# Two-layer graph network on one core: the first dense product and ten chunks of x placed inside the stage that reads R, R in another chunk order, part of the dense R gathered in hop 1

## Chip, cores and metric

The kernel runs on one core of a Trainium2 chip. The metric is the device time of one execution in microseconds (us); lower is better. All data is fp32. The engines are named as in the profile: PE (TensorE, matmul; PEld is its weight load), DVE (VectorE), ACT (ScalarE), POOL (GpSimd), SP (SyncE, which only issues DMAs here).

## The reference

x is 8 x 2048 x 128 (batch, node, feature). adj, called R below, is 2048 x 2048, symmetric in its pattern, with the diagonal full and otherwise about 0.4% of entries set at random, so a 128 x 32 tile of it has few rows that are not zero.

```
# layer 0
sj = x @ w_j;  si = x @ w_i
res = si[:, :, None] + sj[:, None, :] + adj[None] * w_r + g_b
x = layernorm(x + einsum('bij,bjd->bid', res, x) @ weight + bias)
# layer 1: two hops over adj, used as A1 and as A2
x1 = einsum('bnf,nw->bwf', x, adj)
x2 = 2 * einsum('bnf,nw->bwf', x1, adj) - x
out = layernorm(x + relu(concat[x, x1, x2, x1, x2] @ Theta1 + bias))
```

Three products with R are needed: one with R transposed (layer 0), two with R (the hops of layer 1). The outer sum si + sj + b has low rank and is added as a product with nine rows.

## The kernel before

**Blocks.** The 2048 nodes are 16 chunks of 128. A chunk of x or of a result is 128 partitions x 1024 numbers (8 batches x 128 features, 0.5 MiB); a row chunk of R is 128 x 2048 (1 MiB). ND = 4: chunks 0 to 3 are called dense. In layer 0 they are multiplied with the full transposed R, kept on chip in `at4`. For chunks 4 to 15 (and for all 16 in both hops) only the rows that matter are fetched: an index list per 32-column tile ("T", four lists for a chunk) and for the rest ("H", three lists for a chunk). A list is one gather of up to 128 rows of 4 KiB by POOL (`gather`, line 475), so a chunk takes seven gathers. The matching pieces of R have to be gathered too.

**Stage R (lines 294 to 314).** Row chunks arrive in a ring of three buffers `am` (parts of `rc`). For a chunk, PE transposes it in 16 blocks (`row_groups`, 221), ACT writes the result times w_r to `at_of(n)`: `at4` for dense chunks, else one of six buffers in `Y` and `rct`. DVE reduces both forms to masks (`mask_rows`, `mask_columns`). Transposed chunks 4 to 15 are stored to `rr_d` (`store_rt`, 241), 512-byte pieces; chunks 4 to 10 inside the stage, 11 to 15 after it (632). In every second row chunk one chunk of x is transposed (`x_t`) and multiplied with the weights (`y_of`): eight of the 16, the result in `Y`. SP issues from one queue in order: `pump` (199) takes loads from the list `todo`, rows at most three ahead and x at most six ahead.

**After stage R (630 to 661).** For x chunks 8 to 15 PE does `x_t`, `y_of` and two of the 16 steps of the first dense product (`full_rows(0, ...)`, 285; a step is two 128x512 matmuls). In between DVE turns the masks into lists: `ranked(0)` in step n = 9, `candidates` and eight rounds of maxima in step 10, `lists_end(0)` in step 13. `lists_end(0)` gives the T lists, and POOL's first gathers follow it: `get_job` (495) issues one job (R for one chunk and one kind, T four gathers, H three), `keep_job` (510) masks what arrived into `rct` and `rc` on DVE. Jobs run in the order of line 490: T of chunks 6 to 15, 4, 5; H of 4 to 15; then T and H of chunks 0, 1, 2, 3 straight from adj. They pass through a ring of four slots in `st`. The copies of adj's columns to `rr_d` and the 16 stores of `Y` to `y0_d` go through SP's queue after the last chunk of x.

**Dense products 1 to 3 (740 to 809).** PE runs `full_rows(1..3)`. DVE runs the second list extraction, whose rounds (`end_round`, 624) hold one keep and one get each; `lists_end(1)` after the second step of dense product 2 gives the H lists. 22 jobs (all 12 T, ten H: 78 gathers) are issued before the first gather of rows of `y0_d` (`get_rows(0, ND, "T", y0_d)`, 791).

**Sparse loop of layer 0 (812 to 833).** For each chunk c of 4 to 15: seven gathers of `y0_d` into a ring of twelve buffers in `Y`, one keep and one get (here R of the dense chunks, eight jobs of 28 gathers, in c = 4 to 11), own block, rank-9 product, `listed`, then DVE's `z_add` and `layernorm`, and `make_u` of the chunk before, which stores to `u_d`.

**Hops (836 to 903).** Two loops over 16 chunks, with seven gathers each from `u_d` (hop 1) or `y_d` (hop 2); `end` (847) closes a chunk. Every engine keeps its own program order.

Of the kernel before, what the change touches and what calls it, by code (L numbers as in the profile page):

```python
# [11 lines left out]
ALU = mybir.AluOpType  # L12
# [6 lines left out]
def kernel(  # L19
# [22 lines left out]
    P = 128  # L42
# [7 lines left out]
    ND = 4  # L50
# [7 lines left out]
    T_ORDER = list(range(6, NC)) + [4, 5]  # L58
    assert D == P and B == 8 and NC == 16
# [115 lines left out]
    ats = [Y[:, n:n + 2].rearrange("p c b f -> p (c b f)") for n in range(8, NC, 2)]  # L175
    ats += [rct[:, n * N:(n + 1) * N] for n in range(2)]

    def at_of(c):
        t = at4[:, c] if c < ND else ats[(c - ND) % 6]
        return t.rearrange("p (j i) -> p j i", i=P)  # L180

    xin = {}
    todo = []
    for m in range(8):
        todo += [("a", 2 * m), ("x", m)] if m else [("a", 0), ("a", 1), ("x", 0)]
        if m:
            todo.append(("a", 2 * m + 1))
    todo += [("x", n) for n in range(8, NC)] + [("c", c) for c in T_ORDER]
    done = {"a": 0, "x": 0}

    def load_x(c, t):
        sp.dma_start(out=t, in_=x[:, c * P:(c + 1) * P, :].rearrange("b p f -> p b f"))
        return t
# [4 lines left out]

    def pump():
        while todo and (  # L200
            todo[0][0] == "c" or todo[0][1] < done[todo[0][0]] + {"a": 3, "x": 6}[todo[0][0]]
        ):
            what, n = todo.pop(0)
            if what == "c":
                copies([n])
            elif what == "a":
                sp.dma_start(out=am[n % 3], in_=adj[n * P:(n + 1) * P, :])
            else:
                xin[n] = load_x(n, ring[:, n % 6])

    turn = [0]
    turns = [6, 7, 0, 1]
# [8 lines left out]
    def row_groups(n, gs):  # L221
        a, at = am[n % 3], at_of(n)
        for g in gs:
            b = transposes([a[:, (4 * g + i) * P:(4 * g + i + 1) * P] for i in range(4)])
            act.activation(at[:, 4 * g:4 * g + 4, :], b, AF.Copy, scale=wr)
        if gs[-1] == 3:
            done["a"] = n + 1

    def mask_rows(n):
        dve.tensor_reduce(  # L230
            mk[:, n, :], am[n % 3].rearrange("p (t f) -> p t f", f=TW), AX.X, ALU.max,
            apply_absolute_value=True,
        )

    def mask_columns(c):
        dve.tensor_reduce(
            mkt[:, :, QT * c:QT * c + QT], at_of(c).rearrange("p j (t f) -> p j t f", f=TW), AX.X,
            ALU.max, apply_absolute_value=True,
        )
# [4 lines left out]
    def x_t(n):  # L244
        t = []
        for h in range(2):
            b = transposes([xin[n][:, h * HB + i, :] for i in range(4)])
            d = trp[:, (2 * n + h) % 3]
            act.copy(d, b)
            t.append(d)  # L250
        done["x"] = n + 1
        return t
# [40 lines left out]

    pump()
    for m in range(8):
        n = 2 * m
        mask_rows(n)
        row_groups(n, [0, 1, 2, 3])
        pump()
        if ND <= n < NC - 5:  # L300
            store_rt(n)
        if n - 1 >= ND:
            mask_columns(n - 1)
        mask_rows(n + 1)
        row_groups(n + 1, [0, 1])
        xt = x_t(m)
        row_groups(n + 1, [2, 3])
        pump()
        if ND <= n + 1 < NC - 5:
            store_rt(n + 1)  # L310
        y_of(m, xt)
        if n >= ND:
            mask_columns(n)
# [179 lines left out]
    got, kept = [0], [0]  # L493

    def get_job():
        if got[0] == len(jobs):
            return
        what, c = jobs[got[0]]
        s = st[:, got[0] % 4 * BD:]
        got[0] += 1  # L500
        for n, i in enumerate(columns(c, what)):
            if c >= ND:
                gather(
                    s[:, n * 2 * P:(n + 1) * 2 * P], rr_d[c - ND].rearrange("n m f -> n (m f)"), idx,
                    i, N,
                )
            else:
                gather(s[:, n * P:(n + 1) * P], adj128, idr, i, N * NC)

    def keep_job():  # L510
        if kept[0] == got[0]:
            return
        what, c = jobs[kept[0]]
        s = st[:, kept[0] % 4 * BD:]
        kept[0] += 1
        m = 2 if c >= ND else 1
        hc = has[:, columns(c, what)[0]:columns(c, what)[0] + QT]
        for k in range(m):
            if m == 1 or k == 1:
                to = rc[:, c * W:(c + 1) * W]  # L520
            else:
                to = rct[:, (c - ND) * W:(c - ND + 1) * W]
            of = s[:, k * P:]
            if what == "T":
                step = m * P + TW
                dve.tensor_mul(
                    to[:, 0:P].rearrange("p (t f) -> p t f", t=QT),
                    strided(of, QT, step, TW),
                    hc[:, :, None].to_broadcast([P, QT, TW]),
                )  # L530
            else:
                step = m * P + 64
                dve.tensor_mul(
                    to[:, P:2 * P].rearrange("p (t f) -> p t f", t=2), strided(of, 2, step, 64),
                    hc[:, 0:2, None].to_broadcast([P, 2, 64]),
                )
                i = NT + 2 * NC + c
                dve.tensor_scalar(
                    to[:, 2 * P:3 * P], of[:, 2 * m * P:2 * m * P + P], has[:, i:i + 1], None,
                    op0=ALU.mult,  # L540
                )
# [31 lines left out]

    par = [1]

    def acc_pair():
        par[0] ^= 1
        return bank[2 * par[0]:2 * par[0] + 2]
# [52 lines left out]
    acc0 = acc_pair()  # L631
    for c in range(NC - 5, NC):
        store_rt(c)
    for n in range(8, NC):
        xt = x_t(n)
        pump()
        y_of(n, xt)
        if n == 9:
            ranked(0)
        if n in (8, 10, 12):  # L640
            s_rows(2 * (n - 8))
        if n == 10:
            candidates()
            for r in range(8):
                round_of(lists, cand, r)
        if n == 13:
            lists_end(0)
            get_job()
            get_job()
            encode2()  # L650
            get_job()
            get_job()
        if n == 14:
            split2()
        if n == 15:
            candidates2()
            end_round(0)
        full_rows(0, acc0, range(2 * (n - 8), min(2 * (n - 7), 15)))
    assert not todo
    s_rows(12)  # L660
    full_rows(0, acc0, [15])

    zs = {}

    def load_z(c):
        zs[c] = load_x(c, ring[:, 3 + c % 3])

    load_z(0)
    load_z(1)
# [46 lines left out]
    homes = [ring[:, 0], ring[:, 1], ring[:, 2], spare, ring[:, 4], ring[:, 5], ring[:, 3]]  # L716
    homes = [homes[c % 7] for c in range(12)] + [slab(k) for k in range(4)]
# [24 lines left out]
    for r in range(1, 4):  # L742
        end_round(r)
    for c0 in range(0, NC, 4):
        column_sums(c0)
    full_rows(1, acc1, range(4, 6))
    make_ub()
    full_rows(1, acc1, range(6, 12))
    for r in range(4, 8):
        end_round(r)  # L750
    si_t(0)
    rank9(0, acc0)
    z_add(acc0, zs[0])
    full_rows(1, acc1, range(12, NC))
    si_t(1)
    rank9(1, acc1)

    acc2 = acc_pair()
    full_rows(2, acc2, range(0, 2))
# [4 lines left out]
    z_add(acc1, zs[1])  # L764
    layernorm(zs[0], "0_0")
    full_rows(2, acc2, range(2, 8))
# [4 lines left out]
    full_rows(2, acc2, range(8, 12))  # L771
    make_u(0, zs[0], x1t[0], u_of[0])
    load_z(3)
    for _ in range(3):
        keep_job()
        get_job()
    full_rows(2, acc2, range(12, NC))
    si_t(2)
    rank9(2, acc2)
    z_add(acc2, zs[2])  # L780

    acc3 = acc_pair()
    full_rows(3, acc3, range(0, 4))
    make_u(1, zs[1], x1t[1], u_of[1])
    load_z(4)
    for _ in range(3):
        keep_job()
        get_job()
    layernorm(zs[2], "0_2")
    full_rows(3, acc3, range(4, 8))  # L790
# [3 lines left out]
    for _ in range(2):  # L794
        keep_job()
        get_job()
    full_rows(3, acc3, range(8, 12))
    get_rows(0, ND, "H", y0_d)
    keep_job()
    keep_job()  # L800
    get_rows(0, ND + 1, "T", y0_d)
    full_rows(3, acc3, range(12, NC))
# [30 lines left out]
    assert kept[0] == len(jobs)  # L833


    def hop(i, src, order, there, between):
# [51 lines left out]
        for k, c in enumerate(order):  # L888
            rows(k, "H")
            if k > 1:  # L890
                begin(k)
            fetch(k + 2)
            if k > 0:
                rows(k + 1, "T")
            listed(i, c, accs[k], "H")
            end(c, accs[k])

    hop(
        1, u_d, list(range(NC)), range(12, NC),
        lambda: make_u(NC - 1, zs[NC - 1], x1t[NC - 1], u_of[NC - 1]),  # L900
    )
    homes[0:5] = homes[5:10]
    hop(2, y_d, list(range(5, NC)) + list(range(5)), range(5, NC), lambda: None)
# [94 lines left out]
```

## Time and profile before

| | us |
|---|---|
| median of 3 runs | 811.46 (810.09 to 814.63) |
| profiled execution, its own time | 812.94 |
| its span in the profile | 811.0 |
| stage R, last row chunk's mask starts | 94.95 |
| first gather by POOL | 143.19 |
| first gather of rows of y0_d | 254.20 |
| first chunk of the sparse loop added up (z_add, c = 4) | 283.80 |
| last chunk of the sparse loop added up (c = 15) | 432.91 |
| first H gather of hop 1 | 453.94 |
| hop 2, about | 640 to 798 |

Over the span PE is busy 722.5 us (89%), POOL 442.2 (55%), DVE 411.2 (51%), ACT 191.4 (24%); 258.10 MB are moved. POOL's busy time leaves out a gap of about 0.30 us after each gather in which it issues; one gather of about 1.0 us holds POOL for 1.30 us. "DMA" is the mean busy share of the core's 16 DMA engines; by the way it is measured it can pass 1.

### The profile page before, as it was taken

The page shows a single profiled execution, that of the slowest core. Times are in us where ns is not written, and L with a number is a line of the kernel's source. Part 1 is how long each engine was busy: PE and PEld are TensorE (multiplying, and loading weights), DVE is VectorE, ACT ScalarE, POOL GpSimd, SP SyncE. Part 2 cuts the span into 40 slices and gives each one's busy share as a digit, 9 for nine tenths or more (in the row PEclk, how much of TensorE's full clock was granted, in tenths as well). Part 3 has the DMA queues.
Part 4 walks back from the last instruction along what each step waited for, and adds up shares of the span by engine and source line. Part 5 has one row for each costly group of instructions (what it writes and reads, how often), then busy time and mean ns, then how long its engine had stood idle before and what let it go on. Part 6 is the DMA issues. An engine that isn't in the chain of part 4 may idle for free. (4 is left out here: it accounts for less than half of the span.)

```text
span 811.0 us, 10100 instructions
## 1 busy us (share of the span) xinstructions
PE 722.5 (89%) x3566; PEld 373.6 (46%) x3566; DVE 411.2 (51%) x589; ACT 191.4 (24%) x440; POOL 442.2 (55%) x432
## 2 busy tenths in 40 slices
PE   4965699999999998987998799999999899999992
PEld 4865666634345443433444344434444445553441
DVE  4766778698644354543654000000000377777775
ACT  3965644400121232321332100000000011111111
POOL 1000000777577777777644566566663777777640
PEclk9988899999999999999999999999999999999997
DMA  7999999999237799999999899999998799999982
GB/s 251 337 329 316 313 301 316 329 377 399 68 113 257 239 327 351 323 364 328 367 366 323 294 388 382 359 377 344 356 358 344 266 361 351 349 383 379 372 303 71
DMA packets 170036, 258.10 MB, mean 318 GB/s; under 512 B 17409, under 2 KB 122266, under 8 KB 167928
## 3 DMA queue, kind: packets, MB, share of 16 engines
q0 software_dynamic: 49280, 146.52, 49.2%
q1 hardware_dynamic: 97936, 85.21, 32.7%
q10 hardware_dynamic: 22760, 25.63, 9.0%
q8 instruction: 30, 0.49, 0.2%
q14 instruction: 30, 0.25, 0.1%
HBM read 239.01 MB, written 58.72 MB: 367 GB/s over the span
## 5 line engine op out<-in xcount | busy, mean ns | idle before, releaser
L67 POOL DMA_INDIRECT Y<-y_d,idx x196 | 212.0, 1082 | 81.8 <-issue 29.9
L67 PE MATMUL bank<-Y,rc 128*32 128x512 f32 (+2 forms) x896 | 215.7, 607 | 16.1 <-DMA Y<-u_d,idx 12.9
L67 POOL DMA_INDIRECT st<-rr_d,idx x84 | 85.7, 1020 | 172.6 <-DVE rown L67 139.7
L67 POOL DMA_INDIRECT Y<-u_d,idx x112 | 111.7, 998 | 76.7 <-issue 29.1
L67 PEld LDWEIGHTS bank<-Y,rc 128*32 128x32 f32 (+2 forms) x896 | 60.2, 128 | 168.5 <-issue 87.2
L67 PE MATMUL bank<-Y,at 128*128 128x512 f32 x256 | 115.1, 603 | 0.0
L67 PE MATMUL bank<-Y,rct 128*32 128x512 f32 (+2 forms) x336 | 74.8, 604 | 12.9 <-DMA Y<-y_d,idx 12.9
L67 PEld LDWEIGHTS bank<-Y,at 128*128 128x128 f32 x256 | 48.0, 192 | 58.2 <-issue 58.1
L67 DVE TENSOR_REDUCE s<-sq 128x4 f32<-128x512 f32 x64 | 43.9, 686 | 59.4 <-ACT sq L67 59.4
L67 PE MATMUL bank<-ident,rc 128*128 128x128 f32 (+2 forms) x316 | 45.1, 307 | 27.3 <-DMA rc<-in_adj_dram 27.3
L67 ACT ACTIVATE sq<-ring 128x512 f32<-128x512 f32 x54 | 34.0, 630 | 141.2 <-DVE ring L67 94.0
L67 DVE COPY ring<-bank 128x512 f32<-128x512 f32 x10 | 6.9, 692 | 109.0 <-PE bank L67 109.0
L67 PE MATMUL bank<-ring,rd 128*128 128x512 f32 x132 | 62.2, 594 | 0.0
L67 DVE TENSOR_TENSOR ring<-bank,ring 128x512 f32<-128x512 f32 x32 | 21.7, 689 | 67.0 <-PE bank L67 67.0
L67 PEld LDWEIGHTS bank<-ident,rc 128*128 128x128 f32 (+2 forms) x316 | 39.8, 162 | 29.8 <-issue 26.2
L67 DVE TENSOR_REDUCE st<-rc 128x64 f32<-128x2048 f32 x16 | 36.5, 2284 | 31.9 <-DMA rc<-in_adj_dram 31.9
L67 PE MATMUL bank<-th,at 128*128 128x128 f32 x384 | 47.7, 277 | 1.8 <-ACT at L67 1.7
L67 PEld LDWEIGHTS bank<-th,at 128*128 128x128 f32 x384 | 45.3, 192 | 7.9 <-issue 4.2
L67 PEld LDWEIGHTS bank<-Y,rct 128*32 128x32 f32 (+2 forms) x336 | 20.3, 128 | 59.5 <-issue 30.8
L67 ACT COPY ring<-bank 128x512 f32<-128x512 f32 x34 | 19.9, 585 | 114.6 <-PE bank L67 114.6
L67 PE MATMUL bank<-wx,trp 128*128 128x130 f32 x256 | 37.9, 293 | 6.9 <-ACT sraw L67 4.0
L67 PEld LDWEIGHTS bank<-ident,ring 128*128 128x128 f32 x256 | 32.6, 152 | 15.8 <-issue 14.8
(133 smaller groups left out, 788.2 us busy)
## 6 DMA issues: line engine op xcount, KB each, us to landing
rc<-in_adj_dram SPq DMA_DIRECT2D x16, 1024.0 KB, 11.8
ring<-in_x_dram SPq DMA_DIRECT2D x32, 512.0 KB, 9.1
rr_d<-in_adj_dram SPq DMA_DIRECT2D x12, 1024.0 KB, 10.1
ring<-y_d SPq DMA_DIRECT2D x17, 512.0 KB, 8.1
rr_d<-Y SPq DMA_DIRECT2D x8, 1024.0 KB, 9.9
y_d<-Y SPq DMA_DIRECT2D x16, 512.0 KB, 11.5
u_d<-ring ACTq DMA_DIRECT2D x12, 512.0 KB, 7.4
out_dram<-ring ACTq DMA_DIRECT2D x11, 512.0 KB, 8.9
```

The lines of the kernel that those rows point to most:

```text
L67: return lambda *a, **k: tc.keep_in_program_order(f(*a, **k))
```

## The change

Stage R takes the row chunks in the order 0, 4, 5, 6, 1, 7, 8, 9, 2, 10, 11, 12, 3, 13, 14, 15. Ten chunks of x instead of eight are spread over it, and after each but the first one a step of dense product 0 follows. Chunks 4 to 11 are stored in it, 12 to 15 behind it in the SP list, in between the last chunks of x. Five transposed buffers instead of six are used, and transposes use PSUM banks 6, 7, 4, 5. `ranked(0)` moves to n = 11, the first extraction to n = 13; `lists_end(0)` and what followed it move behind the first four steps of dense product 1.

```
+    R_ORDER = [0, 4, 5, 6, 1, 7, 8, 9, 2, 10, 11, 12, 3, 13, 14, 15]
+    NX = 10
+    def x_at(k):
+        m = (k + 1) * NX // NC
+        return m - 1 if m > k * NX // NC else None
+    todo += [("x", 10), ("x", 11), ("s", 12), ("s", 13), ("x", 12), ("x", 13), ("s", 14), ("s", 15)]
+    todo += [("x", 14), ("x", 15)] + [("c", c) for c in T_ORDER[:3]] + [("z", 0), ("z", 1)]
+    todo += [("c", c) for c in T_ORDER[3:]]
...
+    for k, n in enumerate(R_ORDER):
+        m = x_at(k)
+        mask_rows(k)
+        row_groups(k, [0, 1])
+        if m is not None:
+            xt = x_t(m)
+        row_groups(k, [2, 3])
         pump()
-        if ND <= n < NC - 5:
+        if ND <= n < NC - 4:
             store_rt(n)
+        if m is not None:
+            y_of(m, xt)
+            if m:
+                full_rows(0, acc0, [m - 1])
+        if k and R_ORDER[k - 1] >= ND:
+            mask_columns(R_ORDER[k - 1])
...
-    for n in range(8, NC):
+    for n in range(NX, NC):
         xt = x_t(n)
         pump()
         y_of(n, xt)
...
+        if n == 13:
             candidates()
             for r in range(8):
                 round_of(lists, cand, r)
...
+        full_rows(0, acc0, [n - 1])
+        if n < 13:
+            s_rows(4 * (n - NX))
+        if n == 11:
+            ranked(0)
```

Dense R jobs are staged in one buffer, `last`, the third part of `trp`, in place of the four slots; the T form of them is masked with four `tensor_scalar` in place of one `tensor_mul`.

```
+    last = trp[:, 2].rearrange("p i f -> p (i f)")
+    def staged(k):
+        return st[:, k % 4 * BD:] if jobs[k][1] >= ND else last
...
+                for t in range(QT):
+                    at = t * (P + TW)
+                    dve.tensor_scalar(
+                        to[:, TW * t:TW * t + TW], of[:, at:at + TW], hc[:, t:t + 1], None,
+                        op0=ALU.mult,
+                    )
```

The dense part is regrouped. End rounds 0, 1 stand in dense product 1, rounds 2 to 4 and 5 to 7 behind dense products 1 and 2, `lists_end(1)` behind the second step of dense product 3. Of the jobs, 16 (12 T, four H: 60 gathers) are issued before the first gather of `y0_d` and one more before the loop; the loop issues twelve (H of 9 to 15, T and H of 0 and 1, T of 2); the last three (H of 2, T and H of 3: ten gathers) are issued in hop 1.

```
     acc1 = acc_pair()
     full_rows(1, acc1, range(0, 4))
+    lists_end(0)
+    get_job()
+    get_job()
+    encode2()
+    get_job()
+    get_job()
...
+    acc3 = acc_pair()
+    full_rows(3, acc3, range(0, 2))
     lists_end(1)
     for _ in range(2):
         keep_job()
         get_job()
     layernorm(zs[0], "0_0")
+    full_rows(3, acc3, range(2, 7))
     for _ in range(2):
         keep_job()
         get_job()
     layernorm(zs[1], "0_1")
     make_u(0, zs[0], x1t[0], u_of[0])
     load_z(3)
     get_rows(0, ND, "T", y0_d)
...
+            if i == 1 and k % 2 and k < 8:
+                keep_job()
+                if k < 7:
+                    get_job()
             listed(i, c, accs[k], "H")
             end(c, accs[k])
     hop(
-        1, u_d, list(range(NC)), range(12, NC),
+        1, u_d, list(range(ND, 14)) + list(range(ND)) + [14, 15], range(12, NC),
```

Hop 1 takes chunks 4 to 13, then 0 to 3, then 14, 15; hop 2 takes 9 to 13, 0 to 3, 14, 15, 4 to 8. In both kernels eleven chunks of hop 2 and four of hop 1 find their own rows still on chip. The homes of the results and of the `z` chunks in `ring` are renumbered to match.

## The prediction

> **What bounds the kernel now.** I read the page's slices first. The chain of waits that the page prints covers only the last 14 us, so the bound of the stretches that change must come from stages.
>
> ```profile
> POOL 1000000777577777777644566566663777777640
> PEclk9988899999999999999999999999999999999997
> DMA  7999999999237799999999899999998799999982
> ```
>
> DMA is full from the start to 200 us, has a hole of some 60 us, and is nearly full again. POOL starts late. A table of stretches shows the hole (columns: time, then busy us of PE, PEld, DVE, ACT, POOL with instruction counts, granted clock, DMA share, GB/s):
>
> ```profile
> 0.00:95.00 95.00, 61.34 (x409) 56.78 (x410) 60.05 (x52) 57.02 (x131) 2.83 (x12) 0.89 0.99 313
> 95.00:143.20 48.20, 45.00 (x261) 31.09 (x262) 39.86 (x62) 24.18 (x85) 0.01 (x1) 1.00 1.07 301
> 143.20:207.00 63.80, 62.37 (x270) 29.69 (x268) 49.40 (x66) 11.24 (x33) 48.32 (x48) 1.00 1.02 353
> 207.00:254.20 47.20, 44.52 (x142) 22.10 (x142) 25.25 (x65) 10.42 (x19) 31.40 (x32) 0.96 0.36 103
> 254.20:284.00 29.80, 29.34 (x106) 12.91 (x105) 12.60 (x32) 4.84 (x11) 23.13 (x22) 1.00 0.80 282
> 284.00:385.00 101.00, 87.35 (x429) 38.83 (x428) 50.62 (x77) 27.67 (x56) 76.99 (x74) 1.00 0.96 338
> 385.00:433.00 48.00, 46.16 (x243) 21.80 (x242) 27.39 (x40) 15.66 (x31) 23.98 (x24) 1.00 0.96 359
> 454.00:640.00 186.00, 171.28 (x796) 73.39 (x788) 11.92 (x18) 9.36 (x16) 117.30 (x119) 0.99 0.94 347
> ```
>
> Stage R is held by DMA (share 0.99, PE busy 61 of 95 us). From 143 to about 400 POOL is the chain. 74 gathers in 101 us are 1.36 us each, where one alone takes 1.0 and a 0.30 gap. POOL's order of time shows that it hardly rests:
>
> ```profile
> 143.19 1.16 POOL L67 DMA_INDIRECT st<-rr_d,idx  x1 [139.75 <-DVE rown L67]
> ...
> 206.47 1.00 POOL L67 DMA_INDIRECT st<-rr_d,idx  x1 [0.30 <-issue]
> 210.47 1.00 POOL L67 DMA_INDIRECT st<-rr_d,idx  x1 [2.99 <-DVE rc L67]
> ...
> 254.20 1.00 POOL L67 DMA_INDIRECT Y<-y_d,idx  x1 [0.30 <-issue]
> ```
>
> (Rows of y0_d carry the name y_d there.) From 143.19 to 254.20 there are 78 gathers of small R pieces: 78 x 1.30 = 101.6 us and 9.4 of waits. They feed DMA at 103 GB/s only, and the large gathers queue behind them. That is the hole. DVE tells what holds the start, and what a chunk of the loop costs after its gathers:
>
> ```profile
> 121.09 1.09 DVE L67 MAX8 lists<-rc 128x8 f32<-128x896 f32 x1 [3.27 <-ACT rc L67]
> 142.06 0.23 DVE L67 TENSOR_SCALAR has<-bank 128x64 f32<-128x64 f32 x1 [3.66 <-PE bank L67]
> 160.63 2.29 DVE L67 MAX8 lists<-rc 96x8 f32<-96x2048 f32 x1 [5.29 <-ACT rc L67]
> 337.98 0.69 DVE L67 TENSOR_TENSOR ring<-bank,ring 128x512 f32<-128x512 f32 x1 [3.85 <-PE bank L67]
> 347.46 0.28 DVE L67 TENSOR_TENSOR rc<-st,has 128x128 f32<-128x128 f32 x1
> ```
>
> **The change, term by term.** Times are against the profiled execution, 812.94 us (span 811.0 and 1.94 around it), itself 1.48 above the median.
>
> *Stage R.* Before the last row chunk lands, SP now issues one more half-MiB x chunk and one more 1 MiB store: 1.57 MB by 313 GB/s is 5.0 us. The first 20 us show a share of 0.78, so up to 4.4 us of idle DMA could take some, since chunk 4 is stored from the second row on. Bounds +0.6 and +5.0; I take +4, as the loads there wait for ring buffers that the change does not add. Nine steps of dense product 0 move in (two matmuls each, 0.43 us apart in today's order of time: 18 x 0.43 = 7.7 us of PE), and two x chunks of 3.4 us; PE's 95 - 61 = 34 idle us hide both. Without that cover they would be 15 us.
>
> *First lists.* DVE reaches the sums 16.3 us after the last row lands (94.95 to 111.3) and the first add of `ranked` 3.2 us later: 111.3 + 4 + 3.2 = 118.5. The transposes of x 12 want the bank that this add reads, so PE waits until then, with everything behind it: x 12 to 15, the first extraction, `lists_end(0)`. A step of x takes 7.0 us now with eight dense matmuls, so 7.0 - 6 x 0.43 = 4.4. Step 12 ends at 123, x and y of 13 at 126.5, and the extraction starts 2.3 later, as now (118.78 to 121.09): 129, against 121.09. Its rounds take 17.3 us as now: 146.3. PE has by then done steps 13 to 15 and four steps of dense product 1 (143), so that the 3.2 us that DVE now waits for PE (138.4 to 141.6) vanish. POOL starts at 148, +4.8. The SP list could delay it: x 12 stands behind two stores, x 14 behind two more. x 15 comes 7.5 MiB after the last row (seven x chunks, four stores) at 313 GB/s, 25 us, at 124, and is wanted at 133: hidden, with 9 us in hand. Bounds of the start: 0 (no loss in stage R) and +12 (7 us more than forecast).
>
> *Gathers before the large ones.* 60 in place of 78: 18 x 1.305 = 23.5 us less. DVE's second extraction started 18.6 us after `lists_end(0)`; from 146.4 that gives 165, then 37.5 us of rounds and three `z_add` of 1.3: the H lists at 209, while POOL is busy with T jobs until 148 + 62.6 = 210.6. So most of the 9.4 us of waits go too; I leave 2. First large gather: 148 + 78.3 + 2 = 228, against 254.2.
>
> *Start of the loop.* H of chunk 4 is issued by 241; one gather of Y from y_d lands in 7.7 us (part 6 of the profile's page), and PE still has dense product 3's last steps, two `make_u` and the chunk's products. I put the first `z_add` at 255, against 283.8: **-28.8** (bounds -33 and -21, with the start).
>
> *The loop.* Now the first seven chunks take 14.4 us each (283.8 to 384.5, with 10.5 gathers), the last four 12.1 (seven gathers). After the change each has 10 to 11. By POOL 10 x 1.305 = 13.05; by today's row 14.4; I take 14.0 for c = 4 to 11, as the R pieces of H are 128 KB a gather and DMA is at 0.96: 7 x 14.0 - 100.7 = **-2.7** (-9.4 to +2).
> In the last four the one staging buffer makes a new wait: `get_job(c)` on POOL waits for DVE's `keep_job`, which stands behind `layernorm(c - 1)`. Queued behind it on POOL are all gathers of chunk c + 1. From the end of chunk 8's gathers (329.5) to the end of its layernorm (347.5) are 18 us; POOL has 13.7 us of its own work in between. The wait is about 4.3 us where it strikes, and after one the next is small, because POOL is late itself. 4 x 13.7 + 6 = 61 against 48.4: **+12.6** (+6.4 without waits, +24 with a full one each time and slow landing).
>
> *Hop 1.* Ten gathers come in. POOL has 186 - 119 x 1.30 = 31 us free, which hides 13; without this cover it would be 13. DMA has not: 0.66 MB at 347 GB/s is 1.9 us, more in 512-byte pieces, and at the hop's start POOL is behind: **+4** (0 to +15). Its three gets wait for `end(k - 1)`, which POOL's own ring of twelve nearly waits for anyway. The new order of chunks and homes leaves equal counts of loads; I cost it at 0, since eleven and four chunks stay on chip as before.
>
> Sum: -28.8 - 2.7 + 12.6 + 4 = -14.9. On the median: 811.5 - 15 = **797 us**. All bounds together give 811.5 - 36 and 811.5 + 20.
>
> A rule that speaks against a part: the Trainium skill, page "SBUF — State Buffer", section "Who interferes with whom", says that a `tensor_scalar` on VectorE may hold the port pair shared with GpSimd for its whole length, so that GpSimd cannot write DMA descriptors. The change makes 16 small `tensor_scalar` out of four `tensor_mul`. In the trace a gather at 243.66 beside such instructions took 1.08 us, one beside none 1.00. By the skill's rule the cost would be at most 16 x 0.28 = 4.5 us, by the row 16 x 0.08 = 1.3; the sum above holds neither.
>
> **Rivals.**
>
> *DMA is the cap.* With a share of 0.96 in the loop, an earlier start only slows every gather. Then only filled idle time counts: today 47.2 x 0.64 + 29.8 x 0.20 = 36 us idle from 207 to 284; afterwards 19 us (209 to 228) x 0.64 + 27 x 0.20 = 17, and 6 of new waits: 13 gained, 4 paid in hop 1: **803**. For it: DMA in hop 1 stays at 347 GB/s with POOL idle a fifth of the time. Against: 385 to 433 moved 359 GB/s at the same share.
>
> *The single staging buffer decides (slower).* If landings in the crowded loop take 11.1 us (part 6's median for gathers of u_d) and not 7.7, each wait in c = 12 to 15 is 7.7 and does not alternate: 4 x 21.4 - 48.4 = +37; the three gets in hop 1 at the start cost +10. -28.8 + 37 + 10 = +18: **829**. It decides once the last four chunks and hop 1 cost more than 29 us beyond today. Against: POOL stands still during such waits, DMA empties and landings get shorter.
>
> *It does more.* PE could be ready at 250 and DMA go at the 359 GB/s of 385 to 433: -33 - 9.4 + 10 + 2 = -30: **781**.
>
> *It does not start earlier.* If SP's list holds x 15 until 155, then 4.4 for its step, 0.9 and 3.5 for dense steps and 1.6 for the lists put POOL's start at 165, 17 later than forecast, and -15 + 17 = +2: **813**.
>
> **Numbers.** Forecast (787 to 806): 0.58. DMA cap: 0.17. Slower: 0.10. No earlier start: 0.06. More: 0.09. Half a percent, 4 us, is about what a measurement here can tell from no change. Faster takes the forecast, "more" and most of the DMA cap: 0.81; same gets the rest of the cap and two thirds of "no earlier start": 0.07; slower 0.12. The range leaves out the slow end and most of "more": 784 to 811; the forecast's own is 787 to 806.
>
> **What would show it.** Right: POOL's first gather between 143 and 155, first large gather near 228, first `z_add` of the loop near 255, last near 414, hop 1 longer by under 8 us; DMA at 0.36 for some 20 us in place of 47. Wrong: POOL waiting for DVE over 6 us before each dense R gather, the last row chunk landing after 103, or PE waiting for x 14 or 15 after 130.

## The result, and the profile after

Twelve runs of each kernel on the same chip: 814.3 us median before (810.09 to 816.64), 812.25 us after (808.72 to 816.98). The ratio is 0.9984, 95% interval 0.9962 to 1.0006. The change moved a good deal of work and no time that can be measured. The profiled execution has a span of 809.9 us, 1.1 less than before. (Helper lines carry L69 in place of L67.)

The first view of the kernel after is the page's slices:

```profile
POOL 1000000377777776755755577766663777776640
PEclk9998999999989999989999899999999999999997
DMA  7999999998367899998988699999998799999982
```

DMA's hole (the slices 3 and 6) is smaller than before (2, 3, 7, 7), but DMA has new dents behind it. The same stretches as before, with the same columns (time, then busy us of PE, PEld, DVE, ACT, POOL with counts, granted clock, DMA share, GB/s):

```profile
0.00:95.00 95.00, 72.20 (x463) 60.50 (x464) 58.58 (x51) 58.37 (x140) 2.83 (x12) 0.96 0.98 322
95.00:143.20 48.20, 43.36 (x272) 31.55 (x270) 35.83 (x50) 28.08 (x100) 0.00 (x0) 1.00 1.08 308
143.20:207.00 63.80, 62.73 (x242) 27.82 (x241) 51.27 (x75) 5.07 (x10) 41.83 (x42) 1.00 0.92 319
207.00:254.20 47.20, 38.52 (x121) 19.36 (x120) 28.92 (x63) 9.43 (x17) 36.05 (x34) 0.93 0.53 168
254.20:284.00 29.80, 29.11 (x144) 13.97 (x144) 13.92 (x22) 9.68 (x20) 23.39 (x22) 1.00 0.88 279
284.00:385.00 101.00, 93.23 (x460) 42.38 (x457) 54.55 (x96) 29.31 (x59) 67.69 (x65) 0.97 0.96 356
385.00:433.00 48.00, 40.38 (x211) 19.26 (x210) 28.99 (x44) 14.13 (x28) 33.11 (x32) 1.00 0.90 319
454.00:640.00 186.00, 174.25 (x793) 72.32 (x793) 15.02 (x31) 9.38 (x16) 122.86 (x125) 0.98 0.93 342
```

PE's 11 us more in the first stretch are part of the work moved into stage R, at a granted clock of 0.96 in place of 0.89. In the hole DMA's share rose from 0.36 to 0.53; from 143 to 207 it fell from 1.02 to 0.92. POOL's order of time (start, duration, what it issued, idle before it and releaser):

```profile
152.66 1.16 POOL L69 DMA_INDIRECT st<-rr_d,idx  x1 [149.22 <-DVE rown L69]
...
221.29 0.99 POOL L69 DMA_INDIRECT Y<-y_d,idx  x1 [0.31 <-issue]
...
232.83 1.00 POOL L69 DMA_INDIRECT Y<-y_d,idx  x1 [0.30 <-PE bank L69]
```

The large gathers do come early: two at 221 and 223, then from 232.83 on, against 254.20 before. DVE's order of time:

```profile
130.64 1.09 DVE L69 MAX8 lists<-rc 128x8 f32<-128x896 f32 x1 [8.16 <-ACT rc L69]
151.53 0.22 DVE L69 TENSOR_SCALAR has<-bank 128x64 f32<-128x64 f32 x1 [3.58 <-PE bank L69]
171.93 2.29 DVE L69 MAX8 lists<-rc 96x8 f32<-96x2048 f32 x1 [5.51 <-ACT rc L69]
274.94 0.69 DVE L69 TENSOR_TENSOR ring<-bank,ring 128x512 f32<-128x512 f32 x1 [1.34 <-PE bank L69]
386.27 1.29 DVE L69 TENSOR_TENSOR ring<-bank,ring 128x512 f32<-128x512 f32 x2 [7.00 <-DMA ring<-in_x_dram]
```

The first `z_add` of the loop (c = 4) stands at 274.94: 8.9 us earlier than before, where 28.8 were forecast, although the run of large gathers begins 21 us earlier. The last (c = 15) is at 423.45, 9.5 earlier; hop 2 starts at 637.51, 1.1 earlier. So 20 us of the forecast never arrived at the loop, and hop 1 took back nearly all of the 9 that did.

### The profile page after: what moved, and what is told of

Read it like the earlier page. It is cut to its first block, busy times and chain, and to the rows that moved or that the text cites. A ratio compares the mean times of both kernels' runs of the same rounds, so it can differ in the third digit from the quotient of the medians.

```text
span 809.9 us, 10115 instructions
## 1 busy us (share of the span) xinstructions
PE 723.0 (89%) x3566; PEld 368.4 (45%) x3566; DVE 413.6 (51%) x601; ACT 190.7 (24%) x440; POOL 443.6 (55%) x432
## 4 chain that ended last, share of the span: by engine, by line
PE 46%; DMA 32%; issue 8%; POOL 5%; ACT 3%; DVE 3%; POOLq 0%; ACTq 0%; SPq 0%; DVEq 0%
PE bank L69 46%; DMA Y<-u_d,idx 12%; DMA Y<-y_d,idx 8%; DMA ring<-in_x_dram 4%; DMA st<-rr_d,idx 3%; DMA rd<-rr_d 2%; POOL Y L69 2%; POOL st L69 2%; DMA rc<-in_adj_dram 1%; DMA trp<-in_adj_dram,idr 1%; DVE st L69 1%; DVE rc L69 1%; ACT trp L69 1%; ACT Y L69 1%; ACT rct L69 1%
## 5 line engine op out<-in xcount | busy, mean ns | idle before, releaser
L69 POOL DMA_INDIRECT Y<-y_d,idx x196 | 212.4, 1083 | 89.2 <-issue 34.5
L69 PE MATMUL bank<-Y,rc 128*32 128x512 f32 (+2 forms) x896 | 220.3, 614 | 19.5 <-DMA Y<-u_d,idx 17.0
L69 POOL DMA_INDIRECT st<-rr_d,idx x84 | 89.6, 1066 | 176.9 <-DVE rown L69 149.2
L69 POOL DMA_INDIRECT Y<-u_d,idx x112 | 110.9, 990 | 59.6 <-issue 24.4
L69 PEld LDWEIGHTS bank<-Y,rc 128*32 128x32 f32 (+2 forms) x896 | 58.2, 129 | 177.7 <-issue 99.2
L69 PE MATMUL bank<-Y,at 128*128 128x512 f32 x256 | 114.4, 595 | 0.0
L69 PE MATMUL bank<-Y,rct 128*32 128x512 f32 (+2 forms) x336 | 73.0, 624 | 4.3 <-DMA Y<-y_d,idx 4.1
L69 PEld LDWEIGHTS bank<-Y,at 128*128 128x128 f32 x256 | 46.8, 190 | 53.8 <-issue 53.0
L69 DVE TENSOR_REDUCE s<-sq 128x4 f32<-128x512 f32 x64 | 43.9, 686 | 52.0 <-ACT sq L69 52.0
L69 DVE COPY ring<-bank 128x512 f32<-128x512 f32 x10 | 6.9, 692 | 115.8 <-PE bank L69 115.8
L69 PE MATMUL bank<-ring,rd 128*128 128x512 f32 x124 | 59.2, 600 | 7.4 <-DMA rd<-rr_d 7.4
L69 ACT ACTIVATE sq<-ring 128x512 f32<-128x512 f32 x50 | 31.5, 630 | 130.1 <-DVE ring L69 107.6
L69 PE MATMUL bank<-th,at 128*128 128x128 f32 x384 | 49.0, 282 | 7.5 <-ACT at L69 7.4
L69 PE MATMUL bank<-ident,rc 128*128 128x128 f32 (+2 forms) x316 | 42.9, 296 | 12.8 <-DMA rc<-in_adj_dram 12.8
L69 DVE TENSOR_REDUCE st<-rc 128x64 f32<-128x2048 f32 x16 | 36.5, 2283 | 34.4 <-DMA rc<-in_adj_dram 34.4
L69 PEld LDWEIGHTS bank<-th,at 128*128 128x128 f32 x384 | 46.6, 197 | 12.3 <-ACT at L69 9.4
L69 DVE TENSOR_TENSOR ring<-bank,ring 128x512 f32<-128x512 f32 x32 | 21.4, 688 | 59.0 <-PE bank L69 35.9
L69 ACT COPY ring<-bank 128x512 f32<-128x512 f32 x34 | 19.9, 586 | 120.4 <-PE bank L69 120.4
L69 PEld LDWEIGHTS bank<-ident,rc 128*128 128x128 f32 (+2 forms) x316 | 38.3, 156 | 19.3 <-issue 13.3
L69 PE MATMUL bank<-wx,trp 128*128 128x130 f32 x256 | 37.3, 290 | 7.4 <-ACT sraw L69 5.2
L69 PE MATMUL bank<-ident,ring 128*128 128x128 f32 x256 | 36.1, 287 | 7.6 <-DMA ring<-in_x_dram 5.9
L69 PEld LDWEIGHTS bank<-Y,rct 128*32 128x32 f32 (+2 forms) x336 | 20.0, 130 | 49.6 <-issue 35.4
```

The lines of the kernel that those rows point to most:

```text
L69: return lambda *a, **k: tc.keep_in_program_order(f(*a, **k))
```

## The experiments

All eleven runs in one table. The four stretches are read from each profile: first `z_add` of c = 4 | from there to `z_add` of c = 15 (the loop) | from there to the first add of hop 2 | the rest of the span. Ratios are to the kernel before on the same chip.

| run | z_add(4) | loop | hop 1 | rest | median | ratio (95%) |
|---|---|---|---|---|---|---|
| before | 283.8 | 149.1 | 205.7 | 172.4 | 814.3 | |
| after | 274.9 | 148.5 | 214.1 | 172.4 | 812.25 | 0.9984 (0.9962–1.0006) |
| e1_after_cut5 | 271.6 | 148.9 | 214.8 | 172.7 | 810.95 | 0.9967 (0.9940–0.9993) |
| e2_before_cut5 | 282.7 | 149.3 | 208.6 | 171.2 | 813.22 | 0.9997 (0.9973–1.0020) |
| e3_after_x4k | 274.6 | 146.8 | 212.8 | 172.5 | 810.77 | 0.9965 (0.9932–0.9998) |
| e4_after_nohop | 277.2 | 152.3 | 205.3 | 171.8 | 807.64 | 0.9919 (0.9891–0.9947) |
| e5_before_pool_alone | 284.4 | 151.0 | 206.2 | 172.7 | 814.54 | 1.0014 (0.9991–1.0036) |
| e6_after_swap | 268.0 | 151.7 | 215.0 | 173.6 | 808.97 | 0.9930 (0.9903–0.9957) |
| e7_after_early_jobs | 279.5 | 152.7 | 207.0 | 172.3 | 813.69 | 1.0001 (0.9986–1.0015) |
| e8_after_swap_early | 278.5 | 154.8 | 207.5 | 169.5 | 814.35 | 1.0000 (0.9977–1.0023) |
| e9_after_no_x | 277.9 | 133.2 | 216.6 | 170.8 | 796.85 | 0.9791 (0.9761–0.9820) |
| e10_after_dense_behind | 285.2 | 148.5 | 212.6 | 172.5 | 823.92 | 1.0156 (1.0118–1.0193) |
| e11_after_swap_defer | 267.6 | 149.7 | 215.9 | 172.2 | 808.95 | 0.9956 (0.9939–0.9974) |

A stretch comes from one execution and varies by 2 to 4 us where nothing was touched (z_add(4) at 277.2 in e4); a single difference below that is not taken as an effect by itself. Where the text goes into such a difference, it reads waits in the trace, term by term.

### Who sets the start of the loop

**POOL's part of the change alone, in the kernel before.**

```
-    for _ in range(3):        # after make_u(0), and again after make_u(1)
+    for _ in range(1):
         keep_job()
         get_job()
```

The staging of dense R in `last` was taken over with it, and one more keep stands ahead of the loop and one behind it.

> The kernel before the change with one part of the change alone: four H jobs (12 gathers) fewer ahead of the first large gather, 20 instead of 24 jobs issued before the loop, twelve in it, dense R staged in the one buffer as after the change. Theory PE: z_add of c = 4 follows z_add of c = 3 by 11.2 us in both kernels (272.61 to 283.80 and 263.75 to 274.94), all PE work; so POOL's part alone moves the first large gather from 254.2 by 12 x 1.3 = 15.6 us to about 239, but z_add of c = 4 stays within 2 us of 283.8 and the time near 812 to 814. Rival POOL (the prediction's): z_add of c = 4 moves with the gathers, to 268 to 272, and the run is 8 to 12 us shorter.

Measured: one line each of POOL, PE and DVE of this run.

```profile
246.87 1.00 POOL L67 DMA_INDIRECT Y<-y_d,idx  x1 [0.31 <-issue]
```

```profile
250.84 20.77 PE L67 MATMUL bank<-Y,at 128*128 128x512 f32 x48
```

```profile
284.41 0.69 DVE L67 TENSOR_TENSOR ring<-bank,ring 128x512 f32<-128x512 f32 x1 [1.34 <-PE bank L67]
```

The large gathers start 7.3 us earlier and not 15.6. Four gathers of dense R (`trp<-in_adj_dram`) stand ahead of them in the trace, so only eight fewer go out first: the compiled order of POOL's gathers, the one that the trace shows, is not that of the program, here nor in the other kernels. And POOL still waits, 8.62 us in one piece up to 242.97, for DVE's masks, which in turn stand behind a `z_add` (240.81) that waited 11.64 us for PE. `z_add` of c = 4 doesn't move (284.41 against 283.80). PE's row shows why: 48 matmuls of dense product 3 in one piece, 20.77 us. The kernel before has the same piece, from 250.23, and in the 90 us around it PE waits 3.6 us in all, and for no gather (engine and what it waited for: us in total, times, longest):

```profile
PE bank L67 <- DVE miss L67: 1.9, 1, 1.9
PE bank L67 <- ACT sit L67: 1.0, 3, 0.3
PE bank L67 <- ACT at L67: 0.7, 3, 0.2
```

So PE sets the start in the kernel before, and POOL's relief alone moves nothing.

**PE's part alone, in the kernel before.**

```
-    full_rows(3, acc3, range(8, 12))
...
-    full_rows(3, acc3, range(12, NC))
+    full_rows(3, acc3, range(13, NC))
```

> The kernel before the change without five of the 16 steps of dense product 3 (blocks 8 to 12 of the sum for chunk 3 are left out). Theory PE: already here PE set the start of the loop together with POOL, z_add of c = 4 comes 4 to 8.7 us earlier than 283.8. Rival POOL: the first large gather (254.2) and the seven of chunk 4 decide alone, z_add of c = 4 stays within 2 us of 283.8 and the time near 812 to 814.

Measured: PE finishes product 3 5.5 us earlier (`z_add` of c = 3 at 267.07 against 272.61) and then waits for gathers in chunk 4 (PE's order of time, then DVE's):

```profile
278.77 1.98 PE L67 MATMUL bank<-Y,rct 128*128 128x512 f32 x4 [1.35 <-DMA Y<-y_d,idx]
```

```profile
282.72 1.28 DVE L67 TENSOR_TENSOR ring<-bank,ring 128x512 f32<-128x512 f32 x2
```

282.72 against 283.80: my PE theory of 4 to 8.7 us falls, and here the gathers set the start. But they are not the gathers of the kernel before: POOL's compiled order changed too. Four large gathers go out from 231.86 on, and the next eight only from 261.59 to 270.74, where the kernel before issues its first eight from 254.20 to 263.72. So the run shows that PE's relief does not reach the start in this order; how much room the gathers had in the kernel before it does not show. With the median landing time of 7.7 us (part 6 of the page) the eight would have landed near 271.4, an estimate, and PE first uses such rows at 278.91.

**The same steps left out after the change.**

```
-    full_rows(3, acc3, range(7, 12))
```

> The kernel after the change without five of the 16 steps of dense product 3 (row blocks 7 to 11 of the sum for chunk 3 are left out). Theory PE: the loop starts when PE has worked off the dense products, and a step is four matmuls of 0.43 us, so the z_add of c = 4 comes 20 x 0.43 = 8.7 us earlier, near 266 us instead of 274.9. Rival POOL (the prediction's): the start hangs on the gathers, z_add of c = 4 stays within 2 us of 274.9. For the end: if PE's time is what counts, the whole run is 8 us shorter, near 804; if the loop moves its bytes at a fixed rate (51.3 MB at 346 GB/s before and after the change), DMA's idle time ahead of the loop shrinks and only some 2 to 4 us arrive at the end, near 809.

Measured: 271.61, 3.3 us earlier, between the two. First PE's order of time in the kernel after, then in this run:

```profile
223.92 8.85 PE L69 MATMUL bank<-Y,at 128*128 128x512 f32 x20
232.95 1.09 PE L69 MATMUL bank<-ident,ring 128*128 128x128 f32 x8 [0.18 <-DVE ring L69]
240.04 3.48 PE L69 MATMUL bank<-th,at 128*128 128x128 f32 x16 [6.00 <-ACT at L69]
243.35 8.75 PE L69 MATMUL bank<-Y,at 128*128 128x512 f32 x20
253.22 2.05 PE L69 MATMUL bank<-th,at 128*128 128x128 f32 x16 [0.24 <-ACT at L69]
255.10 7.03 PE L69 MATMUL bank<-Y,at 128*128 128x512 f32 x16
270.05 5.71 PE L69 MATMUL bank<-Y,rct 128*32 128x512 f32 x28
```

```profile
239.25 3.42 PE L69 MATMUL bank<-th,at 128*128 128x128 f32 x16 [6.14 <-ACT at L69]
247.59 3.79 PE L69 MATMUL bank<-th,at 128*128 128x128 f32 x16 [4.05 <-ACT at L69]
251.17 7.64 PE L69 MATMUL bank<-Y,at 128*128 128x512 f32 x16
```

The five steps took 8.75 us after the change. Of them 3.8 come back as a second wait for ACT (4.05 in place of 0.24), 3.79 - 2.05 = 1.7 and 7.64 - 7.03 = 0.6 as slower matmuls behind it, and the run was 0.8 early by then: 8.75 + 0.8 - 3.8 - 1.7 - 0.6 = 3.45, against 3.3. So after the change PE's own program sets the start: no gather is waited for up to chunk 4, and what holds PE besides work is its wait for ACT. There `make_u`'s copies stand in ACT's order behind the squares and the root of the next `layernorm`, which wait for DVE.

The rows around that wait also show a clock: 16 matmuls take 3.48 us behind 6.00 us of rest and 2.05 behind 0.24. The granted clock is 0.50 from 237 to 242 us; from 233 to 275 it is 0.92, and 1.00 from 233 to 268 in the run below. The Trainium skill, page "TensorE: Matmul & The Clock Gate", Part 1, says that the array falls to half its clock after an idle window of about 3.4 us and needs as much activity to return; these rows agree. One row of the run below does not: there the clock is 0.50 (282.50 to 284.50) behind a wait of only 2.64 us.

**The wait for ACT taken away.**

```
-    layernorm(zs[1], "0_1")
     make_u(0, zs[0], x1t[0], u_of[0])
     load_z(3)
+    layernorm(zs[1], "0_1")
...
-    layernorm(zs[2], "0_2")
     make_u(1, zs[1], x1t[1], u_of[1])
     load_z(4)
+    layernorm(zs[2], "0_2")
```

> The kernel after the change with make_u(0) ahead of layernorm(zs[1]) and make_u(1) ahead of layernorm(zs[2]); same work. Theory PE: the 6.0 us in which PE waits for ACT's copies, and the 1.4 us by which the 16 matmuls after it are slower, go: z_add of c = 4 at 267 to 268.5 instead of 274.9; the loop takes its 148.5 us by its bytes wherever it starts, so the end moves with it, run near 806. Rival cap: the loop gets longer by what the start gains, as the gathers are no earlier, run near 811 to 812.

Measured, PE's and DVE's order of time:

```profile
234.53 2.05 PE L69 MATMUL bank<-th,at 128*128 128x128 f32 x16 [0.24 <-ACT at L69]
```

```profile
268.00 0.69 DVE L69 TENSOR_TENSOR ring<-bank,ring 128x512 f32<-128x512 f32 x1 [1.34 <-PE bank L69]
268.86 0.69 DVE L69 TENSOR_TENSOR ring<-bank,ring 128x512 f32<-128x512 f32 x1 [0.17 <-PE bank L69]
285.16 0.69 DVE L69 TENSOR_TENSOR ring<-bank,ring 128x512 f32<-128x512 f32 x1 [6.70 <-PE bank L69]
```

The start moves by 6.9 us, as PE's theory has it. But the next chunk comes 17.2 us later in place of 11.8: PE now waits 2.6 us for the gathers of chunk 5, and the matmuls behind this wait run at the lower clock named above. POOL issues without rest here (47 small and large gathers from 233 to 298). The loop takes 151.7, and some 3 us arrive at the end. At 0.9930 of before (0.9903 to 0.9957) it is, with the last run below, the fastest of the kernels that leave nothing out.

**Undoing the first dense product's place.**

```
-            if m:
-                full_rows(0, acc0, [m - 1])
...
+        if n < 14:
+            full_rows(0, acc0, range(2 * (n - NX), 2 * (n - NX) + 2))
+        if n == 14:
+            full_rows(0, acc0, [8])
         full_rows(0, acc0, [n - 1])
```

> The kernel after the change with one part undone: the nine steps of dense product 0 that stand in the stage of R stand behind it again, among x chunks 10 to 14; same work. Theory PE: a step is four matmuls, 1.73 us, so 9 x 1.73 = 15.6 us come onto PE's path, less 1 to 3 us that stage R gets shorter: z_add of c = 4 at 286 to 290 instead of 274.9, run 822 to 826. Rival, the prediction's size of a step (0.86 us): 7.7 us, z_add of c = 4 at 280 to 283, run near 816 to 819.

Measured, DVE's order of time (the sums of `th`, which end stage R, in the kernel after and in this run, then `z_add` of c = 4):

```profile
106.17 1.13 DVE L69 TENSOR_TENSOR th<-th 128x128 f32<-128x128 f32 x4
```

```profile
103.15 1.13 DVE L69 TENSOR_TENSOR th<-th 128x128 f32<-128x128 f32 x4
...
285.20 0.69 DVE L69 TENSOR_TENSOR ring<-bank,ring 128x512 f32<-128x512 f32 x1 [1.34 <-PE bank L69]
```

The start is 10.3 us later, and the run 1.7% longer in the medians' ratios (1.0156 against 0.9984). Stage R's sums start 3.0 us earlier (103.15 against 106.17; the other kernels with this stage unchanged have 104.75 to 107.57), so 13.3 of the 15.6 us of nine steps show; at the prediction's size of a step 7.7 - 3.0 = 4.7 would have. To undo this one part costs more than the whole change gains, so the part pays, and other parts give it back.

### What the loop takes

**x in large pieces.**

```
-            load_z(c + 2)
+            zs[c + 2] = ring[:, 3 + c % 3]
+            sp.dma_start(out=flat(zs[c + 2]), in_=y0_d[(c + 2) * P:(c + 3) * P, :])
```

> The kernel after the change with the nine x loads that are issued inside the loop (c = 6 to 15 less the first) reading rows of y0_d, 128 pieces of 4 KiB in place of 1024 pieces of 512 B, so layer 0 adds other data there. Theory starved queue: SP's small pieces stand behind POOL's backlog, so the four waits of z_add for ring<-in_x_dram (23.2 us) and the 9 us issues of ring<-y_d go, the loop gets 10 to 15 us shorter, run near 799. Rival DMA cap: the bytes are the same and a megabyte on SP's queue costs 2.03% of 148.5 us against 1.8% on POOL's, so 9 x 0.52 MB x 0.25% x 148.5 = 1.7 us shorter, run near 810, with the waits moved to other transfers.

After the change, SP's issue of the own block takes long in the middle of the loop. One line of after, one of before, both in SP's order of time:

```profile
344.12 9.76 SPq L69 DMA_DIRECT2D ring<-y_d  x1
```

```profile
343.71 0.32 SPq L67 DMA_DIRECT2D ring<-y_d  x1
```

With x, which goes in 1024 pieces of 512 bytes, that block lands 20.6 us after its issue (median in the loop; 10.8 before), and DVE waits 23.2 us in four waits of c = 9 to 12. I took this for the lost time. With 4 KiB pieces all four waits are gone and the blocks land in 7.3 us, yet the loop is only 1.7 us shorter, where the starved queue asked for 10 to 15. (That the rival's figure is met to the tenth is luck, as the loop varies by more than that.) The bytes are the same, in a third fewer pieces: neither the waits nor the number of pieces is what holds the loop.

**x left out.**

```
-            load_z(c + 2)
+            zs[c + 2] = ring[:, 3 + c % 3]
```

> The kernel after the change without the nine x loads inside the loop (layer 0 adds old data for chunks 7 to 15; 9 x 0.52 = 4.7 MB of the loop's 51.3 MB are left out). Theory cap: the loop is bound by what DMA moves, 4.7 MB at 346 GB/s are 13.6 us, so z_add of c = 4 to c = 15 takes 135 to 139 us instead of 148.5 (PE's own 134 busy us are the floor) and the run is near 800 to 803. Rival order of waits: the loop is bound by PE, DVE and the ring buffers, only the 23 us of waits for x go and others of the same length come, loop 145 or more, run 809 or more.

Measured: the loop takes 133.2 us in place of 148.5. The table of stretches, one line each of before, after and this run:

```profile
283.80:432.90 149.10, 133.61 (x671) 60.63 (x670) 78.12 (x115) 43.33 (x87) 100.88 (x97) 1.00 0.96 345
```

```profile
274.90:423.50 148.60, 134.28 (x672) 60.76 (x671) 83.12 (x140) 43.58 (x87) 100.64 (x95) 0.98 0.95 345
```

```profile
277.80:411.00 133.20, 128.80 (x672) 60.18 (x671) 83.72 (x139) 43.43 (x87) 94.73 (x94) 0.99 0.94 343
```

The mean rate stays (345, 345, 343 GB/s), the bytes fall (51.3 to 45.7 MB), and the time follows the bytes: 5.6 MB less (the stretch of after holds ten x loads of 0.52 MB) are 16 us at 345 GB/s, and 15.4 are measured. Taken with the run before, which kept the bytes and took the waits away, this shows that the loop's length hangs on the bytes that DMA moves, with PE 10% behind. That the rate of this run is the same is in part chance: up to c = 13 its chunks come every 11.8 us, PE's own pace (PE is busy for 104 of 106 us, at 350 GB/s), and only the last two are slower.

Where the loop starts matters little. In the twelve kernels that leave none of its bytes out, it starts between 267.6 and 285.2 and takes 146.8 to 154.8 us, for 51 to 52.5 MB at 339 to 351 GB/s.

The Trainium skill, page "DMA: Bandwidth & Descriptors", section "Specifications", gives some 358 GB/s as the limit of HBM for one core. The loop's means lie 2 to 5% below it. But the kernel after moves 368 GB/s from 298.50 to 338.20, and single slices of 1/40 of the loop reach 415, so the rows do not show that this limit is what holds the loop.

### What hop 1 takes back

**The last three jobs left out, and issued ahead of the loop.** The first run takes the gets and keeps out of the hop; the second also issues three more jobs before the loop:

```
-            if i == 1 and k % 2 and k < 8:
-                keep_job()
-                if k < 7:
-                    get_job()
...
-    keep_job()
-    get_job()
+    for _ in range(4):
+        keep_job()
+        get_job()
```

> The kernel after the change without the last three jobs in hop 1 (ten gathers of 64 KB and their masks are left out; R lists for H of chunk 2 and for chunk 3 hold old data). Theory waits: the three gets and the keeps cost what hop 1 grew by, first H gather of hop 1 to the start of hop 2 goes from 190.3 back to about 184.7, run 5 us shorter, near 807. Rival bytes: only 0.66 MB at 345 GB/s, 1.9 us, is saved, run near 810. Rival late start: hop 1 grew because chunks come in another order, and nothing changes, near 812.

> The kernel after the change with three more jobs issued ahead of the loop, so that the loop ends the list and none is left for hop 1; same work. Theory PE with costly gets in hop 1: POOL has time to spare before the loop, z_add of c = 4 stays within 2 us of 274.9; the stretch from z_add of c = 15 to the start of hop 2 goes from 214.1 back to about 206 as in the kernel before (205.7) and in the run without these gathers (205.3); run near 807. Rival POOL: the nine gathers delay the large ones by 11.7 us, the start of the loop comes 4 to 10 us later and the run stays near 812.

Measured: without the ten gathers hop 1 takes 205.3 us, as before the change (205.7), against 214.1; the kernels with them took 212.6 to 216.6, and the order of chunks is the new one in all of these. The run is 4.6 us shorter and not 8.8, as its loop starts 2.3 later and takes 3.8 longer in this execution. DVE's copies at the end of chunks show it in the kernel after (POOL issued the four gathers of a job from 483.15 to 487.07):

```profile
476.75 0.69 DVE L69 COPY ring<-bank 128x512 f32<-128x512 f32 x1 [12.44 <-PE bank L69]
...
486.89 0.69 DVE L69 COPY trp<-bank 128x512 f32<-128x512 f32 x1 [9.05 <-PE bank L69]
500.70 0.69 DVE L69 COPY ring<-bank 128x512 f32<-128x512 f32 x1 [13.12 <-PE bank L69]
```

10.1 us, then 13.8 in the chunk with the job; without the jobs 11.2 and 11.5. It is not the bytes: over this stretch the kernel after moves as much as the one before (71.3 against 71.2 MB), at 333 in place of 346 GB/s. PE waits 17.0 us for gathers of `u_d` in it (12.9 before), and the same number of matmuls keeps it busy for 194.3 us (189.3), at a granted clock of 0.97 in place of 0.99. Issued earlier instead, the same jobs make hop 1 short again (207.0), but the loop starts 4.6 later and takes 4.2 longer, and the run is no faster (813.69). The rival's +4 to 10 us at the start is what came; my statement that POOL has time to spare there was wrong.

**Both mends in one kernel, and one more order.**

> Both edits of the two runs before in one kernel, same work as the reference. Theory PE: the gains add, 6 and 5 us, run near 801, ratio to before about 0.985. Rival POOL or cap: the earlier start makes the added gathers count, one of the two gains is lost, run near 806.

Measured: 814.35, a clear miss. The added keeps stand in DVE's order ahead of `layernorm(zs[2])` and `z_add` of c = 3 and wait for R pieces that land late; PE then waits for DVE (first DVE's, then PE's order of time):

```profile
268.54 0.29 DVE L69 TENSOR_SCALAR rct<-st,has 128x128 f32<-128x128 f32 x1 [3.31 <-DMA st<-rr_d,idx]
```

```profile
277.86 1.97 PE L69 MATMUL bank<-ident,ring 128*128 128x128 f32 x8 [6.63 <-DVE ring L69]
```

Both gains are lost. The last run keeps the swap and shifts two jobs from c = 4 and 5 to c = 8 and 9:

```
-        keep_job()
-        get_job()
+        if c > 5:
+            for _ in range(2 if c in (9, 10) else 1):
+                keep_job()
+            for _ in range(2 if c in (8, 9) else 1):
+                get_job()
```

> The kernel of the swap run (make_u ahead of the next layernorm), and the two jobs of c = 4 and 5 are issued in c = 8 and 9; same work. In the swap run POOL never rested from 233 to 298 us and z_add of c = 5 came 17.2 us after that of c = 4. Theory POOL next: six small gathers fewer there, 7.8 us, z_add of c = 5 near 279 instead of 285.2, and up to half of it arrives at the end, run 805 to 808. Rival cap: bytes are only moved within the loop, c = 15 stays at 419 to 421 and the run near 809.

Measured: `z_add` of c = 5 at 282.48 (2.7 earlier than in the swap run, where 6 were expected), but chunk 10 takes 20.1 us (332.08 to 352.16); 808.95 us. It can't be told from the swap run: bytes were only moved within the loop.

## Why the prediction was wrong, by its own steps

**The step that failed: the start of the loop.** The prediction said "From 143 to about 400 POOL is the chain" and "I put the first `z_add` at 255, against 283.8: **-28.8**". It came at 274.9. Its own table had PE busy for 44.5 of 47.2 and 29.3 of 29.8 us there; I read DMA's hole and POOL's unbroken row of gathers, and not that PE was as unbroken. The forecast lets the start follow the gathers and names PE's work ahead of it without a number. e5 shows that POOL's part alone moves nothing, e10 that PE's work moves the start: +10.3 us for nine steps. (In e2, with PE's part alone, a changed order of the gathers took its place.) Relieving POOL by 21 us could gain no more than PE was relieved.

**Under it, a mis-sized term.** "Nine steps of dense product 0 move in (two matmuls each, 0.43 us apart in today's order of time: 18 x 0.43 = 7.7 us of PE)" counts half of what the trace has: 48 matmuls for 12 steps of dense product 3 in 20.77 us, so four of 0.43 us each, 1.73 us a step and 27.7 a product. (A step's two fp32 products are four instructions; the section on the kernel before says two. The prediction itself counts eight matmuls in a step of x, which holds two steps of the dense product.) With the right size PE's remaining work could have been counted: from 232.8 on, nine steps, three `make_u`, the rank products and chunk 4 are 34.7 us (274.94 - 232.83 less 6.0 and 1.4), where the forecast left 27 between 228 and 255. By PE's own rows, its first x chunk behind stage R starts 6.7 us later (100.34 to 107.03), and from there to `z_add` of c = 4 it takes 167.9 us in place of 183.5, 15.6 less: 15.6 - 6.7 = 8.9, the gain of the start. Of the 15.6, nine steps (15.6) and two x chunks (6.8) less the new wait for ACT (6.0) and the slower matmuls behind it (1.4) make 15.0; PE's smaller waits are not in this sum.

**Stage R, +4:** the sums at its end start 4.6 later (101.53 to 106.17), so the number held, by luck. The forecast took it from DMA alone and let PE's idle time hide the moved work. But the last row's mask starts only 1.5 later (96.43), and behind it DVE waits 3.06 us for the last transposed chunk: PE begins to transpose that row at 99.90, after x chunk 8 and its dense step. e10, without the steps in the stage, has the sums 3.0 earlier. So PE's idle time covered most of the moved work, which was 22 us and not 14.5, and not all.

**First lists:** extraction at 130.6 (129 forecast). POOL's first gather at 152.7 and not 148, because DVE's wait for PE at `lists_end(0)` did not vanish (3.58 us): a step of x was 5.3 us, not 4.4, the same half-sized term. H lists at 222 and not 209: DVE waited 6.15 us for PE ahead of the second sum.

**Gathers before the large ones:** the program has 60, as counted. In the trace 52 go out before the first large one at 221.29, four of them for dense R, which the program asks for in the loop; two large ones and six more small ones follow before the others start at 232.83 (228 forecast). Near the forecast, by another order.

**The loop, -2.7 and +12.6:** together +9.9 forecast, -0.6 measured. The first seven chunks took 94.6 us (100.7 before), -6.1; the last four 53.9 (48.4), +5.5. The staging wait is not among POOL's waits there; what stands there is DVE's wait for x (7.00 us at c = 12). Both terms were priced by POOL, while the loop's length hangs on its bytes, which the change leaves as they were.

**Hop 1, +4 (0 to +15):** 8.4 us from the last `z_add` to hop 2, inside its bounds. e4 shows that the moved gathers are the cause, as forecast, but the price is not that of bytes, which grew by 0.1 MB: PE waits for gathers, and its matmuls run slower.

**The rivals.** "DMA is the cap" (803) was right that DMA holds the loop, but not on how the gain goes: the loop did not stretch. "It does not start earlier" has the time (813) by a cause that the trace excludes: PE waits for no x behind stage R. "The single staging buffer" did not strike in the loop; in hop 1 POOL waits for it once, 3.68 us (460.95). "It does more" takes PE as ready at 250, without a row for it. None named PE as the floor of the start, which is the case that came. What the 16 `tensor_scalar` cost POOL was not tested. The sum: -8.9 - 0.6 + 8.4 = -1.1, the difference of the spans.

Open: why the first large gathers are placed where they are in POOL's compiled order, which is not its "own program order" as the section on the kernel before has it, and why the jobs in hop 1 cost PE more than their bytes.

## What to carry over

When an engine's row has no gaps in the stretch that is to shrink, it is a bound, whatever another engine's row looks like: take the smallest relief of all unbroken rows as the gain, not that of the one the change is aimed at. Size the unit of work from a row that holds a known number of them. Where DMA is full, test a stretch with fewer bytes, and with the same bytes and fewer waits: here 11% fewer bytes took 15.4 us off, and 23 us of waits taken away took 1.7.

## What was not expected of the hardware

An SP issue of a 0.5 MB load went from 0.32 to 9 us, and its landing from 10.8 to 20.6 us, with the loop's total rate unchanged at 345 GB/s; in 4 KiB pieces 4.29 us for two issues and 7.3 us to land. The long waits that followed (23.2 us) cost 1.7 us. Ten gathers of 64 KB, 0.66 MB in all and 1.9 us by the rate, cost hop 1 some 8 us (the run 4.6). The clock fell to 0.50 behind a wait of 2.64 us in one run.
